# Redoing the set-up of a two-stage transformer kernel: first tokens' norm pinned first, parameters in a later job, rows spread by DMA

## The chip, the cores and the metric

The kernel runs on one core of a Trainium2 chip. The metric is the device time of one execution in microseconds (us). Five engines work side by side: TensorE (PE, matmuls and transposes; PEld is its weight load), VectorE (DVE), ScalarE (ACT), GpSimd (POOL) and SyncE (SP, which here only issues DMAs). ACT and POOL also issue DMAs. An engine runs its own instructions in program order and waits on semaphores for the others.

## The reference, cut to what matters

Two batches of 2048 tokens with 256 features, all float32. The two stages are modulated by a small condition vector `c`:

```python
mod = (_silu(L0_c) @ L0_wmod).reshape(L0_c.shape[0], 6, 1, -1)
sa, ca, ga, sb, cb, gb = (mod[:, 0], mod[:, 1], mod[:, 2], mod[:, 3], mod[:, 4], mod[:, 5])
ga = (2 * (ga >= 0) - 1) * jnp.maximum(jnp.abs(ga), 0.25)
...
h = _layernorm(x, axis=-1) * (1 + ca) + sa
x = x + ga * _L0_attn_ref(h, ...)      # 3 layers: causal linear attention (random features), MLP
h = _layernorm(x, axis=-1) * (1 + cb) + sb
x = x + gb * _L0_ffn_ref(h, ...)       # 2 layers: windowed softmax attention, gated MLP
```

Of the six modulation vectors, only `sa` and `ca` are needed before the first attention layer. `ga` is first needed when a block of tokens leaves the third layer, `sb` and `cb` just after that, and `gb` in the second stage.

## The kernel before, in words

The first stage (from line 207) cuts each batch into blocks of 256 tokens: 8 blocks for each of 2 batches, 16 in all. A block (`favor_block`, line 664) is loaded (`load_x`, line 214, tile `xin`, three buffers), normed (`normed`, line 344: statistics `bs` and `mv` on DVE, a logarithm and an exponential `rs` on ACT, then `dn` on DVE), turned to feature-major (`turned`, line 361: four PE transposes `ntp`, then ACT applies the modulation and writes `h`), and passes three layers (`favor_layer`, line 396). In a layer, PE makes queries and keys `pq` (line 409) and values `pv` (425), the random features `pu` (448), transposes `tk` (484), scores `sc` (495), state updates `su` (515), the denominator `den` (543), the numerator `nd` (554, 567), the output projection `po` (597), and the MLP `pf` and `acc` (619, 630). The residual `hres` of a layer is `dn` times a row plus a row (`scaled`, line 372, on POOL); these rows are parameters that must stand in all 128 partitions, and they are kept in the tile `brow`: 18 rows of 256 numbers. The second stage (from line 692) follows and is not touched.

What sets the order. PE's instructions in the first stage are put in order by hand: `planned` (line 90) runs up to four blocks as generators at once, always takes the one that is due first, and each `yield` states the PE time of the step and the delay until the next may start. `manual_schedule` at line 688 makes PE keep that order. The other engines' orders are made by the framework's scheduler. In the built program PE's order is: 20 transposes for `brow`, the 24 matmuls of the modulation (`pm`, line 295), 16 more transposes for `brow`, the four `ntp` transposes of each of the first four blocks (0,0), (1,0), (0,1) and (1,1) (batch, block), and only then `pq` of the first block. The third and fourth block's `xin` are loaded by the queue of SP, in which all three layers' weights, 3 MB (3072 KB) each, stand ahead of them (line 246). DMAs of SP and ACT use eight completion semaphores in turn, so a DMA is issued only when the one eight before it has landed.

The set-up in the span of line 224 to 338: `wmod` is loaded in two halves (SP and ACT), then `x` of the first two blocks, then weights; POOL's queue loads `bvb` (a bias row that is repeated over the partitions, 384 KB) and eight small pieces of `om_rep`. The modulation needs `sg` (silu of `c`) and all of `wmod`. `spread` (line 271) widens two parameter rows at a time on DVE, transposes the four pieces on PE, and copies them to `brow` on ACT: nine rounds. `omt` (lines 322 to 338) are feature matrices for three layers on DVE.

Of the kernel before, what the change touches and what calls it, by code (L numbers as in the profile page):

```python
# [39 lines left out]
def block_kernel(ctx: ExitStack, tc: tile.TileContext, t: dict, out: bass.AP):  # L40
# [19 lines left out]
    nc.sync.dma_start(cst, t["consts"])  # L60
# [11 lines left out]
    mhalf = const.tile([P, 16], F32, name="mhalf")  # L72
    nc.gpsimd.memset(mhalf, -0.5)
    mod = const.tile([P, 6, KT, B], F32, name="mod")
    omt = const.tile([P, LA, 2, 4, 2, 8], F32, name="omt")
    bvb = const.tile([P, LA, D], F32, name="bvb")
    nc.gpsimd.dma_start(bvb, t["bv"].partition_broadcast(P))
# [129 lines left out]
    with ExitStack() as c1:  # L207
        wp = c1.enter_context(tc.tile_pool(name="wA", bufs=1))
        psum = c1.enter_context(tc.tile_pool(name="psA", bufs=1, space=PSUM))
        brow = wp.tile([P, NROW, D], F32, name="brow")  # L210
        hp = c1.enter_context(tc.tile_pool(name="hA", bufs=3))
        work = c1.enter_context(tc.tile_pool(name="workA", bufs=2))

# [10 lines left out]
        with tc.tile_pool(name="pro", bufs=1) as pro:  # L224
            wmod = pro.tile([P, KT, 6 * D], F32, name="wmod")
            for kt in range(KT):
                (nc.scalar if kt else nc.sync).dma_start(wmod[:, kt, :], t["wmod"][kt * P : (kt + 1) * P, :])
            early = {b: load_x(b, 0) for b in range(B)}
            om_rep = pro.tile([P, LA, 8], F32, name="om_rep")
            for h in range(8):  # L230
                nc.gpsimd.dma_start(om_rep[16 * h : 16 * h + 16], t["omega"].rearrange("l d m -> d l m"))
            W = {}
            for l in range(LA):
                pool = shared if l < 2 else wp
                wa = pool.tile([P, ROOM], F32, tag=f"wa{l}", name=f"wa{l}")
                wb = pool.tile([P, ROOM], F32, tag=f"wb{l}", name=f"wb{l}")
                for room, at, name, kts, width in (
                    (wa, KT * DFF, "Wq", KT, D),
                    (wa, KT * DFF + KT * D, "Wk", KT, D),
                    (wb, NF * D, "Wv", KT, D),  # L240
                    (wb, NF * D + KT * D, "Wo", KT, D),
                    (wa, 0, "W1", KT, DFF),
                    (wb, 0, "W2", NF, D),
                ):
                    w = room[:, at : at + kts * width].rearrange("p (k n) -> p k n", k=kts)
                    (nc.scalar if (name, l) == ("Wq", 0) else nc.sync).dma_start(
                        w, t[name][l].rearrange("(k p) n -> p k n", p=P)
                    )
                    W[name, l] = w

            cv = vec[:, V_C : V_C + KT * B]
            sg = pro.tile([P, KT * B], F32, name="sg")
            nc.scalar.activation(sg, cv, AF.Exp, scale=-1.0)
            nc.vector.tensor_scalar(sg, sg, 1.0, None, ALU.add)
            nc.vector.reciprocal(sg, sg)
            nc.vector.tensor_tensor(sg, sg, cv, ALU.mult)

            cols = pro.tile([P, NROW, KT], F32, name="cols")

            def col(i, *parts):  # L260
                op = parts[2] if len(parts) > 2 else ALU.add
                if len(parts) == 1:
                    nc.vector.tensor_copy(cols[:, i, :], parts[0])
                else:
                    nc.vector.tensor_tensor(cols[:, i, :], parts[0], parts[1], op)

            def va(l, name):
                o = V_A + l * VA_N + VA[name]
                return vec[:, o : o + KT]

            def spread(lo, hi):
                for i in range(lo, hi, 2):
                    wide = pro.tile([P, 2 * KT, P], F32, tag="wide", name="wide", bufs=2)
                    nc.vector.tensor_copy(
                        wide,
                        cols[:, i : i + 2, :].rearrange("p a k -> p (a k)").unsqueeze(2).to_broadcast(
                            [P, 2 * KT, P]
                        ),
                    )
                    tp = mm_tile("rowtp").rearrange("p (a c) -> p a c", c=P)  # L280
                    for k in range(2 * KT):
                        nc.tensor.transpose(tp[:, k, :], wide[:, k, :], ident)
                    nc.scalar.copy(brow[:, i : i + 2, :].rearrange("p a (k c) -> p (a k) c", c=P), tp)

            for l in range(LA):
                col(R_G1 + l, va(l, "g1"))
                col(R_B1 + l, va(l, "b1"), va(l, "bf2"))
            for l in range(LA - 1):
                col(R_G2 + l, va(l, "g2"))
                col(R_B2 + l, va(l, "b2"), va(l + 1, "bo"))  # L290
            spread(0, R_G0)
            pm = mm_tile("pm")
            for m in range(6 * KT):
                for kt in range(KT):
                    nc.tensor.matmul(
                        pm[:, m * B : (m + 1) * B],
                        wmod[:, kt, m * P : (m + 1) * P],
                        sg[:, kt * B : (kt + 1) * B],
                        start=(kt == 0),
                        stop=(kt == KT - 1),  # L300
                    )
            nc.vector.tensor_copy(mod.rearrange("p a k b -> p (a k b)"), pm[:, : 6 * KT * B])
            for i in (1, 4):
                nc.vector.tensor_scalar(mod[:, i], mod[:, i], 1.0, None, ALU.add)
            for i in (2, 5):
                sgn = pro.tile([P, KT, B], F32, name=f"sgn{i}")
                nc.vector.tensor_scalar(sgn, mod[:, i], 0.0, 2.0, ALU.is_ge, ALU.mult)
                nc.vector.tensor_scalar(sgn, sgn, -1.0, None, ALU.add)
                neg = pro.tile([P, KT, B], F32, name=f"neg{i}")
                nc.vector.tensor_scalar(neg, mod[:, i], -1.0, None, ALU.mult)  # L310
                nc.vector.tensor_tensor(neg, neg, mod[:, i], ALU.max)
                nc.vector.tensor_scalar(neg, neg, 0.25, None, ALU.max)
                nc.vector.tensor_tensor(mod[:, i], sgn, neg, ALU.mult)
            for b in range(B):
                col(R_G0 + b, mod[:, 1, :, b])
                col(R_B0 + b, mod[:, 0, :, b], va(0, "bo"))
                col(R_GE + b, va(LA - 1, "g2"), mod[:, 2, :, b], ALU.mult)
                col(R_BE + b, va(LA - 1, "b2"), mod[:, 2, :, b], ALU.mult)
            spread(R_G0, NROW)


            for hf in range(2):
                own, other = slice(64 * hf, 64 * hf + 64), slice(64 - 64 * hf, 128 - 64 * hf)
                for l in range(LA):
                    nc.vector.tensor_tensor(
                        omt[own, l, hf].rearrange("p h s m -> p (h s) m"),
                        om_rep[own, l, :].unsqueeze(1).to_broadcast([64, 8, 8]),
                        hm2[own, 8 * hf : 8 * hf + 8].unsqueeze(2).to_broadcast([64, 8, 8]),
                        ALU.mult,
                    )  # L330
                    nc.vector.tensor_scalar(omt[own, l, hf], omt[own, l, hf], 0.5, None, ALU.mult)
                    nc.vector.tensor_scalar(
                        omt[other, l, hf].rearrange("p h s m -> p (h s m)"),
                        nhalf[other, 64 - 64 * hf : 128 - 64 * hf],
                        0.25,
                        None,
                        ALU.mult,
                    )

        rp = c1.enter_context(tc.tile_pool(name="rA", bufs=2))  # L340
        fp = c1.enter_context(tc.tile_pool(name="featA", bufs=2))
        sp = c1.enter_context(tc.tile_pool(name="smallA", bufs=2))
# [45 lines left out]
        nc.vector.tensor_reduce(par, hmask.rearrange("p (i q) -> p q i", q=2), AX.X, ALU.add)  # L388
# [5 lines left out]
        turn = [0]  # L394

        def favor_layer(b, n, l, h, hres):
# [45 lines left out]
            yield 5.2, 0.6, "attention"  # L442
            feat = []
# [171 lines left out]
            for f in range(NF + 1):  # L615
                if f < NF:
# [9 lines left out]
                    fr[f] = fp.tile([P, TA], F32, tag="fr", name="fr", bufs=3)  # L626
# [37 lines left out]
        def favor_block(b, n):  # L664
            dn = normed(early.pop(b) if n == 0 else load_x(b, n))
            yield 0.0, 4.0
            h = hp.tile([P, KT, TA], F32, tag="h", name="h0")
            turned(dn, h, lambda k: mod[:, 1, k, b : b + 1], lambda k: mod[:, 0, k, b : b + 1])
            hres = scaled(dn, R_G0 + b, R_B0 + b)
# [18 lines left out]
        with tc.manual_schedule(engines={mybir.EngineType.PE}):  # L688
            planned([favor_block(b, n) for n in range(S // TA) for b in range(B)], 4)
# [628 lines left out]
```

## Time and profile before

| | |
|---|---|
| median of 3 runs | 3013.61 us (3012.41 to 3014.05) |
| the profiled execution | 3012.11 us, of which the span from first to last instruction is 3010.3 us |
| PE busy | 2927.8 us (97%) |
| DVE, ACT, POOL busy | 1679.1 us (56%), 1345.9 us (45%), 1065.0 us (35%) |
| mean granted TensorE clock | 0.992 |
| DMA, whole span | 57.10 MB, mean 19 GB/s |
| DMA, 0 to 50 us | 275 GB/s, busy share 0.81 |
| PE busy, 0 to 50 us | 26.29 us |
| PE busy, 50 to 100 us | 47.96 us |

How to read it: "busy" is time in instructions; "idle before" is the gap ahead of an instruction and what ended it. The clock is the share of full speed that the throttle granted to TensorE. In the list of DMAs, "us to landing" is from issue to the moment that the last byte is confirmed. In the chain of waits each row is a start, a length, and an engine with tile and line, or a DMA, that the end of the program hung on.

### The profile page before, as it was taken

The numbers are of one execution on the slowest core, as the hardware profiler recorded it, in microseconds if no ns is written. First come the engines' busy times: TensorE is split into PE (matmuls) and PEld (weight loads), VectorE is DVE, ScalarE is ACT, GpSimd is POOL, SyncE is SP. The second block draws the span as 40 slices with busy tenths as digits, with TensorE's granted clock in tenths as the row PEclk, the third lists the DMA queues.
The fourth block names the chain that finished last, engine by engine and source line by source line (L and its number), as shares of the span: only waits on it lengthen the run. The fifth ranks groups of instructions, "written<-read, shape, count | busy, mean of one in ns | idle before, by whom it ended". The sixth has DMA issues, their size and how long they took to land.

```text
span 3010.3 us, 49194 instructions
## 1 busy us (share of the span) xinstructions
PE 2927.8 (97%) x19356; PEld 2138.0 (71%) x19356; DVE 1679.1 (56%) x4178; ACT 1345.9 (45%) x3269; POOL 1065.0 (35%) x937
## 2 busy tenths in 40 slices
PE   6999999999999999999996999999999999999999
PEld 5788888888888888788883777775444777776444
DVE  5555565555565555655544777774224777774222
ACT  3333343334443343433333667665114667665211
POOL 2222233222332223322224666663002666663000
PEclk9999999999999999999997999999999999999999
DMA  5000010000100001001012000001000000000011
GB/s 183 1 1 1 1 39 19 1 1 1 36 22 1 1 1 36 22 1 43 16 41 76 1 2 1 1 2 57 0 0 10 20 1 2 1 1 8 28 42 35
DMA packets 37288, 57.10 MB, mean 19 GB/s; under 512 B 3693, under 2 KB 28609, under 8 KB 36545
## 3 DMA queue, kind: packets, MB, share of 16 engines
q1 hardware_dynamic: 36176, 52.37, 5.3%
q8 instruction: 153, 2.51, 0.3%
q0 software_dynamic: 464, 0.54, 0.1%
q10 hardware_dynamic: 416, 1.05, 0.1%
q14 instruction: 79, 0.64, 0.1%
HBM read 41.37 MB, written 12.58 MB: 18 GB/s over the span
## 4 chain that ended last, share of the span: by engine, by line
PE 89%; DVE 4%; ACT 3%; POOL 2%; DMA 1%; issue 1%; SPq 1%; ACTq 0%; DVEq 0%; POOLq 0%
PE acc L630 10%; PE pf L619 10%; PE pqkv L785 10%; PE pg L1130 5%; PE acc L1164 5%; PE pq L409 5%; PE pa L1130 4%; PE av L974 4%; PE sim L881 3%; PE ptp L948 3%; PE po L993 3%; PE sc L495 3%; PE nd L567 3%; PE pu L448 3%; PE pv L425 3%; PE po L597 3%
## 5 line engine op out<-in xcount | busy, mean ns | idle before, releaser
L630 PE MATMUL acc<-wb,fr 128*128 128x256 f32 x1536 | 397.3, 381 | 5.5 <-ACT fr L627 5.1
L619 PE MATMUL pf<-h,wa 128*128 128x256 f32 x1536 | 400.2, 384 | 1.1 <-ACT h L370 0.7
L627 ACT ACTIVATE fr<-pf,vec 128x256 f32<-128x256 f32 x384 | 180.5, 471 | 425.6 <-PE pf L619 424.9
L785 PE MATMUL pqkv<-wqkv,s 128*128 128x512 f32 x768 | 357.9, 602 | 8.2 <-issue 8.2
L501 DVE TENSOR_TENSOR att<-sc,cst 128x512 f32<-128x512 f32 x384 | 238.4, 683 | 157.5 <-PE sc L495 157.5
L630 PEld LDWEIGHTS acc<-wb,fr 128*128 128x128 f32 x1536 | 287.8, 190 | 52.1 <-ACT fr L627 8.6
L379 POOL TENSOR_TENSOR res<-dn,brow 128x512 f32<-128x512 f32 x112 | 144.8, 1292 | 485.4 <-DVE dn L356 483.8
L619 PEld LDWEIGHTS pf<-h,wa 128*128 128x128 f32 x1536 | 275.8, 190 | 55.8 <-issue 19.5
L936 POOL TENSOR_TENSOR pm<-pm,sum 128x1024 f32<-128x1024 f32 (+1 forms) x128 | 235.8, 1842 | 178.2 <-DVE sum L931 178.2
L921 ACT ACTIVATE pm<-pm,mx 128x256 f32<-128x256 f32 (+1 forms) x512 | 249.5, 489 | 58.2 <-DVE mx L913 57.0
L785 PEld LDWEIGHTS pqkv<-wqkv,s 128*128 128x128 f32 x768 | 138.0, 193 | 135.8 <-issue 133.9
L1139 DVE SCALAR_TENSOR_TENSOR ge<-pa,vec,ge 128x512 f32<-128x512 f32 x80 | 60.1, 751 | 298.1 <-PE pa L1130 249.7
L827 POOL TENSOR_TENSOR rot<-raw,rsn_wo 128x512 f32<-128x512 f32 x128 | 160.5, 1275 | 185.4 <-ACT raw L808 185.4
L1138 ACT ACTIVATE ge<-pg,vec 128x512 f32<-128x512 f32 x96 | 65.9, 687 | 325.1 <-PE pg L1130 325.1
L421 ACT ACTIVATE xs<-xs 64x512 f32<-64x512 f32 x192 | 120.7, 629 | 152.1 <-DVE xs L420 142.7
L1130 PE MATMUL pg<-s,w 128*128 128x512 f32 (+1 forms) x384 | 182.2, 597 | 0.0
L1164 PE MATMUL acc<-ge,w 128*128 128x512 f32 (+1 forms) x384 | 182.0, 596 | 0.0
L409 PE MATMUL pq<-h,wa 128*128 128x256 f32 x768 | 175.3, 381 | 0.0
L420 DVE TENSOR_TENSOR xs<-pq,vec 64x512 f32<-64x512 f32 x192 | 132.2, 689 | 76.4 <-PE pq L409 72.6
L409 PEld LDWEIGHTS pq<-h,wa 128*128 128x128 f32 x768 | 146.1, 191 | 21.1 <-issue 1.4
L849 POOL TENSOR_TENSOR qk<-qk,rot 128x1024 f32<-128x1024 f32 x64 | 151.5, 2368 | 0.5
L1130 PE MATMUL pa<-s,w 128*128 128x512 f32 x320 | 150.4, 592 | 0.0
(162 smaller groups left out, 5362.6 us busy)
## 6 DMA issues: line engine op xcount, KB each, us to landing
xin<-in_x_dram SPq DMA_DIRECT2D x32, 256.0 KB, 2.8
x<-res SPq DMA_DIRECT2D x16, 256.0 KB, 2.1
h<-hm SPq DMA_DIRECT2D x16, 256.0 KB, 2.4
s<-h SPq DMA_DIRECT2D x16, 256.0 KB, 5.6
xl<-x SPq DMA_DIRECT2D x8, 512.0 KB, 4.4
out_dram<-res SPq DMA_DIRECT2D x8, 512.0 KB, 3.2
w<-in_w_dram SPq DMA_DIRECT2D x6, 640.0 KB, 4.0
wa<-in_W_dram SPq DMA_DIRECT2D x3, 1024.0 KB, 9.7
```

The costliest lines, as they stand in the source:

```text
L409: nc.tensor.matmul(pq[:, g, :], W[wn, l][:, kt, g * P : (g + 1) * P], h[:, kt, :], start=(kt == 0), stop=(kt == KT - 1),)
L501: nc.vector.tensor_tensor(am, scs[i].rearrange("p g q c -> p (g q) c"), caus.unsqueeze(1).to_broadcast([P, 2 * KT, P]), ALU.mult,)
L619: nc.tensor.matmul(pf, W["W1", l][:, kt, f * P : (f + 1) * P], h1[:, kt, :], start=(kt == 0), stop=(kt == KT - 1),)
L627: nc.scalar.activation(fr[f], pf, AF.Relu, bias=v("bf1", f))
L630: nc.tensor.matmul(acc[:, c, :], fr[f - 1][:, c * P : (c + 1) * P], W["W2", l][:, f - 1, :], start=(f == 1 and c == 0), stop=(f == NF), sk ...
L785: nc.tensor.matmul(pq, s[:, kt * TB + c * P : kt * TB + (c + 1) * P], wqkv[:, kt, i * INNER : (i + 1) * INNER], start=(kt == 0), stop=(kt ...
L827: nc.gpsimd.tensor_tensor(rot[:, :, :, lo : lo + 32], got["raw"][:, :, :, hi : hi + 32], rsn[:, ti, :, lo : lo + 32].unsqueeze(2).to_broad ...
L849: nc.gpsimd.tensor_tensor(got["qk"], got["qk"], got["rot"], ALU.add)
L921: nc.scalar.activation(pm[:, hd, :], pm[:, hd, :], AF.Exp, bias=of("mx", hg)[:, hd : hd + 1], accum_out=of("sum", hg)[:, hd : hd + 1],)
L936: nc.gpsimd.tensor_tensor(pm, pm, of("sum", hg).unsqueeze(2).to_broadcast([P, 4, kw]), ALU.mult)
L1130: nc.tensor.matmul(pt[:m, :], w1[:, kt, off : off + m], hb[:, kt * TB : (kt + 1) * TB], start=(kt == 0), stop=(kt == KT - 1),)
L1164: nc.tensor.matmul(acc[m], w2[:w, f, m * P : (m + 1) * P], g[:w, :], start=(f == 0), stop=(f == NFH - 1),)
```

## The change

The set-up is split in three.

First, `first_norm` is a fixed order of PE, DVE and ACT: `sg`, the eight matmuls that make `sa` and `ca` alone, the parameter columns, the norm of block (0,0), its four transposes, its `h`, two transposes for `brow`, `omt` of the first layer. What `planned` orders is held behind the end of that (`issue_after`).

Second, `rest_of_setup` is one more job of `planned`, in second place among the blocks. It holds the other 16 modulation matmuls, in four steps between the blocks' steps, `omt` of the other two layers, the sign and magnitude of `ga` and `gb`, the last four `brow` rows, and the loads of the third layer's weights, which took their place in SP's queue after the second layer's before.

Third, `spread` no longer widens: one transpose turns up to 20 columns into rows, ACT copies them, POOL's DMA stores them to DRAM, and a second DMA of POOL reads them back with each row repeated over the 128 partitions (4 KB and 10 KB per partition at the start, 512 KB and 1280 KB in all; 4 KB, 512 KB, later).

Loads: SP now issues the identity's 64 KB of `consts` alone, then `x` of the first two blocks, then the rest. ACT's queue loads the first third of `wmod` (512 KB), Wq and Wv of the first layer. The other two thirds of `wmod` (1 MB) follow the first layer's W1 on SP. On POOL `om_rep` comes ahead of `bvb`. `wmod` and the staging tile stand in the room that the third layer's weights use later; so these loads wait for the last modulation matmul, and for the store of the last rows. `hres` of a block's first layer is made after `pv` instead of ahead of `pq` when the block is the first of its batch.

In the built program PE's order is now: 8 `pm`, 4 `ntp` of (0,0), 2 transposes for `brow`, `pq` and `pv` of (0,0), then 8 `ntp` of (1,0) and (0,1), `pu` of (0,0), 4 `pm`, `tk`, `sc`, `su`, 8 `pm`, `sc`, `den`, 4 `pm`, `nd`, and so on. The `ntp` of (1,1) stand beside those of the first block's MLP input, and one transpose for `brow` follows the second block's `pu`. Behind that, PE's order is the same as before, instruction by instruction. On SP, `xin` of block (0,1) follows the second layer's weights.

```diff
-            for kt in range(KT):
-                (nc.scalar if kt else nc.sync).dma_start(wmod[:, kt, :], t["wmod"][kt * P : (kt + 1) * P, :])
-            early = {b: load_x(b, 0) for b in range(B)}
...
+        nc.scalar.dma_start(wmod[:, :, : 2 * D], wmod_in[:, :, : 2 * D])
+        early = {b: load_x(b, 0) for b in range(B)}
+        nc.sync.dma_start(cst[:, P:], t["consts"][:, P:])
...
+        load_weights(0, "Wq", "Wk", "Wv", "Wo")
+        load_weights(0, "W1")
+        nc.sync.dma_start(wmod[:, :, 2 * D :], wmod_in[:, :, 2 * D :])
+        load_weights(0, "W2")
+        load_weights(1, "Wq", "Wk", "Wv", "Wo", "W1", "W2")
...
+        def spread(lo, hi):
+            n = (hi - lo) * KT
+            tp = mm_tile("rowtp")[:n, :P]
+            nc.tensor.transpose(tp, cols[:, lo:hi, :].rearrange("p a k -> p (a k)"), ident)
+            turned_ = turned_cols.pop()[:n]
+            nc.scalar.copy(turned_, tp)
+            nc.gpsimd.dma_start(rows_out[lo * KT : hi * KT], turned_)
+            nc.gpsimd.dma_start(
+                brow[:, lo:hi, :].rearrange("p a d -> p (a d)"),
+                rows_out[lo * KT : hi * KT].rearrange("a c -> (a c)").partition_broadcast(P),
+            )
...
+        def first_norm(normed, turned):
...
+                pm = mm_tile("pm")
+                condition(0, 2, pm)
...
+                dn = normed(early.pop(0))
+                conditioned(0, 2, pm)
+                h = hp.tile([P, KT, TA], F32, tag="h", name="h0")
+                turned(dn, h, lambda k: mod[:, 1, k, 0:1], lambda k: mod[:, 0, k, 0:1])
...
+                spread(R_G0, R_GE)
+                spread(0, R_G0)
+                omega_rows(0)
...
+        def rest_of_setup():
+            yield 0.0, 8.0, "mlp"
+            pm = psum.tile([P, NCA * D], F32, tag="acc", name="pm2", bufs=1)
+            for i in range(2, 6):
+                condition(i, i + 1, pm)
+                yield 1.7, 0.0, "mlp"
+            conditioned(2, 6, pm)
...
+            yield 0.0, 2.5
+            spread(R_GE, NROW)
+            load_weights(2, "Wq", "Wk", "Wv", "Wo", "W1", "W2")
+            yield 0.2, 0.0
...
+            with tc.issue_after(last_first):
+                planned(blocks[:1] + [rest_of_setup()] + blocks[1:], 4)
```

## The prediction, made before the run

> **What bounds the kernel now.** I read the page first: PE is busy for 97% of the span, and of its 40 slices of 75 us only the first and one at the stage change are poor. The change touches the start alone, and behind it PE's order is the same, so what counts is how soon PE gets going for good. The table of busy times by stretch shows where the start is lost (columns: stretch, length, busy us and instructions of PE, PEld, DVE, ACT, POOL, then clock, DMA share, GB/s):
>
> ```profile
> 20.00:25.00 5.00, 4.52 (x22) 4.43 (x21) 0.41 (x3) 0.00 (x0) 0.00 (x0) 1.00 1.07 376
> 25.00:30.00 5.00, 2.79 (x13) 2.62 (x14) 4.27 (x33) 1.57 (x4) 0.00 (x0) 1.00 1.09 352
> 30.00:35.00 5.00, 2.49 (x13) 1.71 (x11) 3.26 (x6) 2.48 (x6) 3.75 (x5) 0.96 1.06 381
> 35.00:40.00 5.00, 0.07 (x1) 0.00 (x0) 0.55 (x2) 1.02 (x2) 3.09 (x3) 0.50 0.87 278
> 40.00:45.00 5.00, 1.70 (x5) 0.87 (x5) 4.34 (x11) 2.02 (x6) 3.48 (x3) 0.50 0.19 54
> ```
>
> The DMA engines are full until 38 us (one-microsecond stretches show it), while no engine is. PE idles from 35 to 42 us. The chain of waits says for what:
>
> ```profile
> 26.29 0.71 SPq L246
> 27.04 12.39 DMA xin<-in_x_dram
> 39.45 0.75 DVE bs L349 x2
> ...
> 45.52 0.90 PE ntp L366 x3
> 46.42 4.42 PE pq L409 x16
> 50.84 1.79 PE pv L425 x8
> 52.63 2.04 PE pu L448 x16
> 54.69 0.61 ACT ft L458
> 55.34 0.66 PE tk L484 x4
> 55.99 1.07 PE sc L495 x16
> 57.07 1.09 PE su L515 x8
> 58.16 2.60 PE sc L495 x16
> ```
>
> The chain does not run through the modulation or `brow`. It runs through the load of `x` of the third block, (0,1), issued at 27.04 behind 9 MB of weights and landed at 39.45. Blocks (0,0) and (1,0) had been transposed by 35 us, but PE's order has all four blocks' `ntp` ahead of the first `pq`. From 46.42 on PE hardly stops: 47.96 of the 50 us from 50 to 100.
>
> **The change, part by part.** First what vanishes from PE's start: 36 transposes become 3 and the first norm needs 8 of the 24 `pm` matmuls. In the timeline the first 20 transposes end at 14.5, the `pm` take 10.24 us to 24.5 and the last 16 transposes 3.65 us from 27.21. All of that lies beside the loads, so shortening it gains nothing by itself. DVE's widening and ACT's nine copies likewise. In the new order, `h` of (0,0) should stand at about 10 to 12 us: `vec` landed at 4.55 before, 256 KB of `x` come early in the queue, and norm, 8 `pm` (3.4 us) and transposes (0.9 us) follow. Then `pq` and `pv` run by about 18 us instead of 46 to 52.6.
>
> Then PE stops. Next in its order are `ntp` of (1,0), which is ready, and of (0,1), whose `x` still stands behind two layers' weights on SP. So the same load is late next; call its landing T. I compare the moment when `pu` of (0,0) starts: 52.63 before.
>
> T: the third layer's 3072 KB (3.146 MB) no longer stand ahead of it. At the rate of 20 to 35 us (376, 352, 381: mean 370 GB/s) that is 8.5 us. Added are POOL's two repeated rows, 1792 KB (1.835 MB) of DMA. Their issue: `brow` columns are copied by about 11 us, POOL is through its 8 `om_rep` issues (0.59 us each), `bvb` and two 1.84 us memsets by then; the store lands some 5 to 7 us later (`om_rep` took 5.5 to 7.8), and the reading back runs from about 20 to 30 us, inside the wait for T. Here a rule speaks against the change. In the stretches when `bvb`, the like transfer, moved beside SP's and ACT's, the rates were 401, 230 and 283 GB/s (5 to 8 us; mean 305). The Trainium skill, "DMA: Bandwidth & Descriptors", section "Issuing engines are not separate DMA queues", says that DMAs issued on POOL end up on the same 16 DMA engines and interleave with the others. The row agrees: the third queue raised no total. By the rule the repeat is paid by T; were POOL's queue apart, it would cost nothing. Its price: by the mean of the nearest stretch 1.835/0.305 = 6.0 us; at best 5.0 (370 GB/s); at worst 8.0 (230). I take 6.0. Moving `wmod`, Wq, Wv, `consts` and `om_rep` changes no bytes ahead of T. T = 39.45 - 8.5 + 6.0 = 36.95, say 36.9.
>
> From T to `pu`: statistics, logarithm, exponential and first half of `dn` took 2.0 us before (39.45 to 41.42), then four transposes at half clock 1.2 us: 3.3 with a semaphore. `pu` starts at T + 3.3.
>
> What PE does behind it, beyond before: 16 `pm` matmuls, two passes each, at 10.24/48 = 0.213 us: 6.8 us. Four stand between `pu` and `tk`, where PE waited 0.69 us for `ft` (timeline), eight between `su` and the second `sc`, which took 2.60 instead of 1.07 since DVE had to free its PSUM. So 0.7 + 1.5 is cover and 4.6 us is paid; without the cover it would be 6.8. The transpose for `brow` hides in the same wait of the second block, the `ntp` of (1,1) in the 0.66 us wait for `h` at 78.07. But DVE norms (1,1) just ahead of that: two statistics (0.74) before the first block's `dn`, whose transposes PE waits for; cover 0.5: 0.2 us paid, at most 0.8.
>
> Clock: PE idles from about 18 us to T + 2, so its clock falls, as it did at 34.8 before. Before, dense work started at 45.5 and the clock was back at 48.2; that fell on `pq` (4.42 instead of 3.65 us). Now it falls on `ntp`, `pu` and `pm`. The Trainium skill, "TensorE: Matmul & The Clock Gate", Part 1, has the clock restored after a busy window of about 3.4 us that runs free. By the row 2.7 us at half clock cost 1.35; by the rule, as an estimate, the restart can miss a window and wait up to two, 6.8 us, which costs 3.4. I take 4.1 us at half clock, 2.05 us, of which 0.45 is in the transposes already: 1.6.
>
> Other steps at nothing: 18 small DVE instructions of the later job (0.07 us apart, 1.3 us) stand ahead of `aT`, while PE has the second block's `pq` and `pv` (5.4 us). POOL's store of the last rows waits for ACT's copy; behind it stand `res` and the second block's `z`, wanted by `den` at 82.03: z ended at 77.25, `res` takes 2 times 1.27, issue 0.5, so 1.5 us remain. The reading back waits on POOL for the store (5 us); behind it are `res` and state updates, wanted much later. The third layer's loads now wait on SP for the last `pm` and that store, about 75 us; behind them is one `x` of a later block end, and a POOL addition waits for that to about 80, before POOL's next `z`, wanted at about 101. The weights themselves are first used at 263.9.
>
> Sum: gain = 52.63 - (36.9 + 3.3) - 4.6 - 0.2 - 1.6 = 6.0, i.e. 43.0 - T with rounding. The profiled execution, 3012.1 (span 3010.3), would fall to 3006.1; the median of the runs, 3013.6, stands 1.5 above it, so I forecast 3007.6. The sum rounds at the border of what the measurement can tell, 0.2% or 6 us.
>
> **The rivals.** *POOL's repeat costs T nothing*, because its bytes fill gaps or end outside the wait. For: two queues together reached 413 GB/s at 3 to 4 us, more than SP's alone. Against: the DMA share lies at 1.0 to 1.1 from 8 to 38 us, so there are no gaps. T = 30.9, gain 12.1: 3001.5. Chance 0.18.
>
> *The room is taken up again*: `x` of (0,1) still lands at 39 to 42, by small rows of `wmod` and slower interleaving. For: the fall to 230 GB/s beside POOL. Gain 1 to 4: 3011. Chance 0.11.
>
> *It is not what PE waits for*: if PE needed only the first block, it would go on from 18 us. Gain 52.6 - 18 - 4.6 = 30: 2984. The order with `ntp` of (0,1) ahead of `pu` speaks against it. Chance 0.02.
>
> *Slower*: POOL's large pieces (8 or 16 rows' worth against SP's 1 KB) take two thirds of the engines' time, and repeating one DRAM row is slow: `bvb` needed 7.5 us to landing for 384 KB, which makes 35 us of 1792 KB. SP's last 4 MB at 20 us would then run at a third of 370 GB/s: 33 us, T = 53, 10 us slower: 3024. It decides from T = 43 on (no gain), and is over 0.2% slower from T = 49. Against it: while `bvb` moved, the total was never below 230 GB/s. Chance 0.04.
>
> The likeliest, T between 35.5 and 39.4, has 0.65: 3006.1 to 3010.
>
> **How the numbers follow.** Within the likeliest case the price of the repeat (5 to 8), the clock (0.9 to 2.9) and DVE's 0.8 put the gain at 3.5 to 7.5, half of it on each side of 6. Faster: 0.35 + 0.18 + 0.02 = 0.55. Same: 0.30 + 0.11 = 0.41. Slower: 0.04. The range takes in the first rival and the slow end: 3001.5 to 3010.5; outside remain the small mishaps, 30 us of gain and the slow case.
>
> **What would show it.** Right: `pq` of (0,0) before 20 us, then PE idle to T + 2 with `xin` on the chain; T near 37; the clock at half from the low 20s to about 42; `pu` near 40; second `sc` without its wait; the same gaps from 100 us on; the third layer's loads near 55 and 75 us with nobody waiting. Wrong: T at 31 or over 40; a wait of PE for `brow` or `res` at `po`; a gap at `den` by a late `z`; or PE stopped before `pq` by Wk or `om_rep`.

## The result, and the profile after

The changed kernel takes 3008.73 us (median of 22 runs, 3005.76 to 3013.69), the kernel before 3013.80 in the same comparison (22 runs, 3009.94 to 3015.80): a ratio of 0.9984, 95% interval 0.9977 to 0.9990, or 5.1 us. The profiled execution took 3008.91 us (span 3007.1, mean granted clock 0.989), 3.2 us less than the profiled one of before. The runs of the changed kernel are spread by 8 us, and the spread goes with the mean granted clock: 0.990 in the three at 3006, 0.986 in the one at 3013.7.

The same five stretches as before, from the changed kernel's table of busy times by stretch, in the same columns:

```profile
20.00:25.00 5.00, 0.10 (x1) 0.00 (x0) 0.60 (x2) 1.06 (x3) 0.00 (x0) 0.90 1.06 393
25.00:30.00 5.00, 0.00 (x0) 0.00 (x0) 0.00 (x0) 0.00 (x0) 0.00 (x0) 0.50 1.02 396
30.00:35.00 5.00, 0.00 (x0) 0.00 (x0) 0.55 (x2) 0.00 (x0) 0.00 (x0) 0.50 0.94 297
35.00:40.00 5.00, 3.42 (x16) 2.10 (x18) 1.15 (x5) 1.86 (x5) 3.16 (x3) 0.50 0.21 53
40.00:45.00 5.00, 5.00 (x47) 3.58 (x44) 4.71 (x4) 1.44 (x3) 4.91 (x4) 0.89 0.01 3
```

The modulation, the first norm, and `pq` and `pv` of block (0,0) are done by 19.7 us. Then every engine stands still for about 15 us while the DMA engines stay full. The chain of waits says for what, and what it costs to start again:

```profile
17.91 16.51 DMA xin<-in_x_dram
34.45 0.75 DVE bs L408 x2
...
36.58 1.13 PE ntp L425 x4
37.71 3.56 PE pu L510 x16
41.27 0.98 PE pm L310 x8
...
44.91 1.68 PE pm L310 x16
46.59 3.44 PE sc L557 x15
50.03 2.00 PE den L605 x4
52.04 1.50 PE pm L310 x8
53.54 1.86 PE nd L629 x32
55.40 1.15 PE nd L616 x4
56.55 1.80 PE nd L629 x32
58.35 3.65 PE pq L469 x16
...
74.03 1.96 PE pf L681 x8
...
83.38 3.65 PE pq L469 x16
```

The same part of the chain before the change, from `den` of (0,0) on:

```profile
60.75 1.06 PE den L543 x4
61.81 1.01 PE nd L567 x32
62.83 0.64 PE nd L554 x4
63.47 1.01 PE nd L567 x32
64.48 3.65 PE pq L409 x16
...
78.07 2.02 PE pf L619 x8
...
87.48 3.65 PE pq L409 x16
```

It is still the load of `x` of block (0,1), now landed at 34.45 instead of 39.45, and `pu` of (0,0) starts at 37.71 instead of 52.63. But of this lead of 14.9 us only 6.1 are left at the next block's `pq` (58.35; 64.48 before), and 4.0 at the first block's `pf` (74.03; 78.07). At `pq` of (0,1) the lead is 4.1 (83.38; 87.48). So 10.9 us are given back within 40 us, and the experiments have two questions: what set T, and where the 10.9 went. Compare lengths in the two chains: `pu` takes 3.56 instead of 2.04, the second `sc` 3.44 instead of 2.60, and `nd` 4.81 (three rows) where before had 2.66 (1.01, 0.64, 1.01). The clock fell a second time, from 47.9 to 58.2, in the midst of what is recorded as busy work.

One line of the chain explains itself only in the timeline of DVE and POOL. First the changed kernel, from the start of POOL's residuals (start, length of the group, count, idle before):

```profile
36.84 2.49 POOL L438 TENSOR_TENSOR res<-dn,brow 128x512 f32<-128x512 f32 x2 [18.87 <-DVE dn L415]
40.29 1.95 DVE L526 TENSOR_SCALAR qe<-ft,par 128x512 f32<-128x512 f32 x2 [3.54 <-ACT ft L520]
42.16 3.37 DVE L532 TENSOR_TENSOR_SCAN z<-ft,zero 128x256 f32<-128x256 f32 x2
```

Then the same two steps of DVE in the kernel before, where POOL was idle beside them:

```profile
54.52 0.88 DVE L464 TENSOR_SCALAR qe<-ft,par 128x512 f32<-128x512 f32 x2 [1.10 <-ACT ft L458]
55.32 1.27 DVE L470 TENSOR_TENSOR_SCAN z<-ft,zero 128x256 f32<-128x256 f32 x2
```

POOL's order has the residual of block (0,1) first, which needs that block's norm. So all residuals run behind T, from 36.84 to 45, and beside them DVE needs 5.3 us instead of 2.1 for the two steps that PE's scores wait for.

### The profile page after: what moved, and what is told of

The parts are those of the page before. It is cut to its first block, busy times and chain, and to the rows that moved or that the text cites. A ratio compares the mean times of both kernels' runs of the same rounds, so it can differ in the third digit from the quotient of the medians.

```text
span 3007.1 us, 49118 instructions
## 1 busy us (share of the span) xinstructions
PE 2926.8 (97%) x19323; PEld 2135.3 (71%) x19323; DVE 1677.9 (56%) x4170; ACT 1341.0 (45%) x3263; POOL 1068.9 (36%) x942
## 4 chain that ended last, share of the span: by engine, by line
PE 89%; DVE 4%; ACT 3%; POOL 2%; issue 1%; DMA 1%; SPq 0%; ACTq 0%; POOLq 0%; DVEq 0%
PE acc L692 11%; PE pf L681 10%; PE pqkv L854 10%; PE pg L1199 5%; PE acc L1233 5%; PE pq L469 5%; PE pa L1199 4%; PE av L1043 4%; PE sim L950 3%; PE ptp L1017 3%; PE po L1062 3%; PE sc L557 3%; PE nd L629 3%; PE pu L510 3%; PE po L659 3%; PE pv L485 3%
## 5 line engine op out<-in xcount | busy, mean ns | idle before, releaser
L692 PEld LDWEIGHTS acc<-wb,fr 128*128 128x128 f32 x1536 | 288.4, 190 | 52.6 <-ACT fr L689 8.6
```

Of the source, the lines that this page charges most:

```text
L692: nc.tensor.matmul(acc[:, c, :], fr[f - 1][:, c * P : (c + 1) * P], W["W2", l][:, f - 1, :], start=(f == 1 and c == 0), stop=(f == NF), sk ...
```

## The experiments

My theory ("waits"): T is set by SP's queue and by POOL's repeat; what is lost behind `pu` is PE waiting for DVE, which POOL slows. The rival ("thin"): the 16 small `pm` matmuls in the stream are what costs, by their own time and since they keep TensorE too little occupied, so that the clock falls again. Each experiment edits the changed kernel, and each comparison has its own runs of the kernel before (medians 3014.1 to 3014.4 us; 3013.8 for the changed kernel). Where a run is called faster than the changed kernel, the two medians are subtracted, so half a microsecond of it can be the comparison.

**Is the gate T, and nothing else?** `x` of (0,1) is issued right behind the first two.

```diff
-        early = {b: load_x(b, 0) for b in range(B)}
+        early = {(b, 0): load_x(b, 0) for b in range(B)}
+        early[0, 1] = load_x(0, 1)
...
-                dn = normed(early.pop(b) if n == 0 else load_x(b, n))
+                dn = normed(early.pop((b, n)) if (b, n) in early else load_x(b, n))
```

> The changed kernel, with the load of x of block (0,1) issued on SP directly behind the x of the first two blocks, ahead of all weights; PE's order stays. If that load is what PE waits for (gate), its statistics start at 9 to 12 us instead of 34.45, pu of (0,0) at 20 to 22 instead of 37.7, and everything behind it 14 to 17 us earlier; the time falls from 3008.7 to 2993 to 2997. If weights or the rows in brow are what PE needs next anyway, PE stops again at pu, po or pf until 30 to 35 us and the gain is 5 us or less.

Measured: 2990.81 us, ratio 0.9922 (0.9909 to 0.9934): 17.9 us faster than the changed kernel, somewhat more than I expected. Its chain of waits has no `xin` any more:

```profile
16.89 7.61 DMA brow<-rows_out
24.64 2.50 POOL res L439 x2
...
30.40 1.23 POOL z L543
31.67 2.07 PE den L606 x4
```

`pu` starts at 19.6, and what is late next is the repeat: the residuals wait for `brow` until 24.64, POOL's `z` stands behind them, and PE's `den` waits for it. The gate is shown.

**What does the repeat cost T?** The reading back is replaced by a constant, so the parameter rows are left out.

```diff
-            nc.gpsimd.dma_start(
-                brow[:, lo:hi, :].rearrange("p a d -> p (a d)"),
-                rows_out[lo * KT : hi * KT].rearrange("a c -> (a c)").partition_broadcast(P),
-            )
+            nc.gpsimd.memset(brow[:, lo:hi, :], 1.0)
```

> The changed kernel without POOL's repeating read into brow: a memset of 1.0 on POOL stands in its place, so the rows of parameters are left out. If the 1792 KB are paid by the wait for the third x, its landing falls from 34.45 by 5 us (4 to 6) to about 29.5, and the time by as much. If POOL's bytes fill gaps, the landing stays within 1 us of 34.45.

Measured: 3004.60 us (3001.15 to 3006.58), ratio 0.9966 (0.9953 to 0.9978). In its chain of waits, the third `x` landed at 29.62 instead of 34.45:

```profile
29.62 0.75 DVE bs L405 x2
```

So 1.835 MB cost T 4.8 us, 382 GB/s, and not nothing; in the time 4.1 us.

**Are the small matmuls the loss?** The 16 `pm` stand behind `pv`, where PE is idle.

```diff
-            yield 0.0, 8.0, "mlp"
+            yield 0.0, 3.0, "mlp"
...
                 condition(i, i + 1, pm)
+            yield 0.1, 1.3, "mlp"
+            for _ in range(4):
                 yield 1.7, 0.0, "mlp"
```

> The changed kernel, with all 16 later modulation matmuls together behind pv of (0,0), where PE waits for the third x anyway; PE's order is else the same. pu of (0,0) should stay at 37.7. Theory thin (matmuls of two columns count as little activity, and that is why the clock falls again at 48 us): no second fall, pq of (1,0) at about 51 instead of 58.4, 7 us faster. Rival waits (the second fall comes from PE's waits for DVE's att): the clock falls again, pq of (1,0) at 54 to 55, about 4 us faster. If the matmuls were covered, nothing changes.

Measured: 3007.99 us (14 runs, 3004.23 to 3010.03), ratio 0.9979 (0.9971 to 0.9987): 0.7 us under the changed kernel, which is not clear of the spread. In the median both expectations missed. The profiled execution, 3004.52, is one of the three fastest, and it looks otherwise. Its chain of waits, then its stretch from 50 to 55 us and that of the changed kernel (the clock is the third number from the end):

```profile
37.50 3.64 PE pu L512 x16
...
52.60 3.65 PE pq L471 x16
```

```profile
50.00:55.00 5.00, 5.00 (x79) 4.21 (x76) 2.11 (x4) 1.32 (x2) 0.00 (x0) 1.00 0.01 3
50.00:55.00 5.00, 5.00 (x45) 4.45 (x44) 3.11 (x20) 1.32 (x2) 0.00 (x0) 0.50 0.05 11
```

The clock came back later than in the changed kernel (45.9 instead of 41.1) and then did not fall again, as "thin" had it, though DVE's two steps took 1.96 and 3.36 us beside POOL. `pq` of (1,0) starts at 52.60, between the two expectations. Whether the clock fell in the executions near the median is not known, since none of them was traced.

**Is it POOL beside DVE?** The residual of (0,1), too, is made after `pv`, so that the other blocks' residuals on POOL no longer wait for T.

```diff
-            if n > 0:
+            if n > 1:
                 hres = hres()
```

> The changed kernel, with the first residual of block (0,1) too made only when that block reaches it, so POOL's first res no longer waits for dn of (0,1); those of (0,0) and (1,0) can run while PE waits for x. Theory waits: qe and z on DVE no longer run beside POOL (1.95 and 3.37 us become about 0.9 and 1.3), att starts 2.5 to 3 us earlier, the second fall of the clock at 48 us does not come, 4 to 5 us faster. Theory thin: att comes earlier, but the clock still falls near 48 us, gain at most 1.5 us.

Measured: 3005.49 us (10 runs, of which nine at 3005.05 to 3007.11), ratio 0.9975 (0.9965 to 0.9984): 3.2 us faster than the changed kernel, somewhat under what "waits" gave. The profiled execution was the tenth, 3013.98: its clock stayed at half from 21.7 to 62.6, so its trace doesn't stand for the median.

**Does a warm clock help?** Two tries with matmuls that nobody reads. Fourteen of 512 columns behind `pv`:

> The changed kernel with 14 matmuls of 512 columns, whose result nobody reads, behind pv of (0,0): about 12 us of PE's 16 us wait for the third x at full clock, so no work is added to the path. Theory clock (the start that the change gains is partly lost because PE comes back at half clock and stays there, for the lone first block gives it too little to do): pu takes 2.0 instead of 3.6 us, most of the half-clock time between 37 and 58 us goes, pq of (1,0) starts 3 to 6 us earlier than 58.4 and the time falls by 3 to 6 us. Rival (the half clock costs little, the rest is waits and the 16 small matmuls): at most 1.5 us.

Measured: 3009.46 us (21 runs), ratio 0.9985 (0.9978 to 0.9991). This tells nothing: the matmuls ran from 19.60 to 31.78, PE came back at 36.9, and the clock had fallen again at 34.4 (`pu` 3.43 us). Then the same fourteen together with the 16 `pm` behind `pv`:

> The 16 later modulation matmuls moved into PE's wait for the third x, as in the run that moved them alone (which gained 0.7 us in the median), and the 14 unread matmuls behind them. Theory clock: moving them gained so little because PE then stayed at half clock longer; with the clock kept up pq of (1,0) starts at 49 to 51 instead of 58.4, 7 to 9 us faster than the changed kernel. Rival: no more than the moved matmuls alone, 1 to 2 us.

Measured: 3008.26 us (16 runs), ratio 0.9977 (0.9969 to 0.9984), 0.5 us under the changed kernel. They ran until 37.04 and made `pu` 1.8 us late, but it ran at full clock (1.95 us). Yet with a warm clock and no small matmul in the stream PE waited for `ft` (0.70), `qe` (0.50) and `att` (1.63), since DVE's two steps again took 1.98 and 3.28 us beside POOL. The second `sc` took 3.86, and the clock fell at 48.2, as in the changed kernel:

```profile
47.14 3.86 PE L565 MATMUL sc<-qe,ft 32*128 32x256 f32 x16 [1.63 <-DVE att L571]
```

So the second fall does not need the small matmuls, against "thin". Nor are DVE's slow steps enough for it: in the profiled execution with `pm` behind `pv` alone they were as slow.

**Is it the norm of (1,1) between `pu` and `pf`?** Its start is put off.

```diff
-            yield 0.2, 0.0
+            yield 0.2, 6.0
```

> The changed kernel with the start of block (1,1) put off by 6 us of planned time, so that DVE norms it after the first block's MLP input. If DVE's norm of (1,1) is what keeps PE at 65 to 74 us, pf of the first block follows pu of the second by 6.5 us as before the change, not by 8.6, and the time falls by about 2 us. If PE only finds another wait, nothing changes within 1 us.

Measured: 3008.73 us (21 runs), ratio 0.9984 (0.9978 to 0.9991), the changed kernel's own. The profiled execution took 3013.07, with the clock at half from 21.5 to 62.5, ahead of the part that matters here. From `pu` of (1,0) to `pf` it is still 8.1 us (6.5 before, 8.6 in the changed kernel). The edit moved the transposes of (1,1) behind `pf` in PE's order, but not the norm of (1,1) in DVE's order, where half of it still stands ahead of `att`:

```profile
75.17 1.37 DVE L415 TENSOR_SCALAR dn<-xin,mv,rs 128x256 f32<-128x256 f32 x1 [0.60 <-ACT rs L412]
76.46 2.47 DVE L563 TENSOR_TENSOR att<-sc,cst 128x512 f32<-128x512 f32 x4
77.24 1.97 PE L681 MATMUL pf<-h,wa 128*128 128x256 f32 x8 [2.29 <-issue]
```

The profile names no releaser for `pf`, but the kernel's text does: `pf` and the scores `sc` take turns in the same four buffers of PSUM, the memory that PE writes to (lines 553 and 679 of the changed kernel), and a buffer comes free when an `att` has read its scores. In the changed kernel and in all twelve variants of it, `pf` starts 0.77 to 0.78 us after DVE starts `att`, whose first instruction takes 0.69. Before the change `att` started 2.05 us ahead of `pf` (76.02), which waited for ACT's `h`. And from `pu` to ACT's `h` the changed kernel takes 5.94 us, the same as before, so all of the 2.1 us lie behind `h`. The expectation fell because the edit didn't put off what it was meant to put off; the wait is for DVE, which comes late to `att`.

**Both cures of the loss together.** `pm` behind `pv`, and the late residual of (0,1).

> On the changed kernel, both cures together: the 16 matmuls of the modulation stand in PE's long wait behind pv, and the residual of block (0,1) is made later, so that POOL works less beside DVE. If what is lost behind pu is PE's wait for DVE beside POOL plus the small matmuls, the two gains add: the clock does not fall a second time, pq of (1,0) starts near 51 instead of 58.4, and the time is 3000 to 3003. If the clock falls again by the luck of its windows whatever is waited for, or PE waits for the next engine instead, it is about 3005, as with the late residual alone.

Measured: 3002.96 us (3002.03 to 3003.90), ratio 0.9965 (0.9952 to 0.9977): 5.8 us faster than the changed kernel, where the two alone gave 0.7 and 3.2. DVE's steps in the timeline, with POOL idle beside them:

```profile
40.03 0.88 DVE L528 TENSOR_SCALAR qe<-ft,par 128x512 f32<-128x512 f32 x2 [3.54 <-ACT ft L522]
41.74 1.27 DVE L534 TENSOR_TENSOR_SCAN z<-ft,zero 128x256 f32<-128x256 f32 x2 [0.82 <-ACT ft L522]
```

and its chain of waits:

```profile
37.45 3.64 PE pu L512 x16
...
44.58 2.59 PE sc L559 x16
47.17 1.06 PE den L607 x4
48.23 1.01 PE nd L631 x32
...
50.90 3.65 PE pq L471 x16
...
64.27 2.71 DVE dn L417 x2
67.67 1.97 PE pf L683 x8
```

The lengths are those of before (`sc` 2.6, `den` 1.06, `nd` 1.01) except `pu`, which runs at half clock. From `pu` to the next `pq` it takes 13.45 us: before 11.85, in the changed kernel 20.64; the 1.6 that remain are `pu`'s. The expectation is borne out, to the place (51 expected, 50.90) and the time, and the two cures give more together than the 3.9 us of their sum. Since both causes are out, this run does not tell them apart. Behind it 3.2 us are still lost to `pf`: there DVE's two `dn` of (1,1) take 2.71 us, beside two products on POOL that take 3.32.

**The cold restart by itself.** The late residual, `pm` where they were, and 18 unread matmuls, which last until PE goes on.

> On the changed kernel with the late residual (3005.5): 18 matmuls of 512 columns whose result nobody reads are put into PE's wait behind pv, 0.87 us each at half clock, from 19.6 to about 35, so that the clock has been restored when PE goes on. If the cold restart costs what the chain shows (pu 3.6 instead of 2.0, transposes 1.1 instead of 0.5, the rest behind waits), 2 to 3 us are gained: 3002.5 to 3004. If the work behind pu is bound by DVE and ACT anyway, nothing is gained: 3005 to 3006.

Measured: 3002.76 us (3001.05 to 3003.30), ratio 0.9962 (0.9950 to 0.9975): 2.7 us faster than the late residual alone. In its chain of waits:

```profile
37.22 1.88 PE pu L517 x16
...
50.01 3.65 PE pq L476 x16
```

The clock stays up from 15.8 to 67.0 in its trace; the unread matmuls took 0.87 us each at full clock, not at half as I had written. So the cold restart costs 2.7 us. And the 16 `pm` are in the stream here, 3.45 us of them; from `pu` to `pq` it takes 12.8 us against 11.85 before, so with DVE free of POOL they cost 0.9.

This kernel and the one with fourteen unread matmuls and `pm` behind `pv` set the two theories against each other with the clock up when `pu` starts. With DVE beside POOL and no small matmuls in the stream, `pu` to `pq` takes 17.1 us, the second fall of the clock included, and the time is 3008.26 (lowest 3003.66); with the small matmuls and DVE free, 12.8 us and 3002.76 (highest 3003.30). Of the 5.5 us between the times, 2.3 are the later start of `pu` there. "Waits" names the larger part of the loss.

**A better kernel?** On top of the early `x`, three tries to get POOL's `z` from behind the residuals: the late residual of (0,1); the residual of (0,0) made only just ahead of `po`; both.

> Third x ahead of the weights and the first residual of (0,1) made late, together. With the third x early, the chain runs over POOL: z of (0,0) waits in POOL's queue behind residuals that wait for brow (24.6 us). With fewer residuals ahead of z, den of (0,0) starts 2 to 3 us earlier than 31.7, so 2988 to 2990 against 2990.8. If POOL's first residual waits for brow all the same, no change within 1 us.

> The early third x (2990.8), and the first block's residual made only just ahead of po. In the kernel with the early x, POOL's z of (0,0) started at 30.36 behind four residual steps that waited for the repeated rows until 24.64, and PE waited 3.69 us for it at den. One residual's steps of 2 times 1.26 us are still ahead of z in POOL's order, and a state that waits for DVE's sum at 27.2: den starts about 1 us earlier (30.5), the time is about 2989.7. If PE waits for something else instead, 2990.8.

> As the one before, and the residual of block (0,1) is late too: only one step of 1.26 us and the state stand ahead of z on POOL. By POOL's order den starts at 29.2 instead of 31.67, 2.5 us earlier: 2988.3. If the residuals that are now later slow DVE's norm, as they did with the late residual on the early x (2992.6), the gain is lost again behind den: 2990 to 2992.

Measured: 2992.57, 2991.12 and 2993.49 us; ratios 0.9928 (0.9915 to 0.9942), 0.9925 (0.9911 to 0.9938) and 0.9933 (0.9921 to 0.9946). None beats the early `x` alone. `den` did come earlier: 30.88, 31.50 and 29.25 instead of 31.67. The last kernel's chain of waits shows how that is lost:

```profile
29.25 2.08 PE den L604 x4
...
49.48 3.31 POOL res L439 x2
52.82 2.75 DVE dn L416 x2
```

The residuals that were put off now run beside DVE's norms, and `pf` starts at 56.3 against 55.3.

Where the kernels stood, by the start of PE's groups in their traces:

| | `pu` (0,0) | `pq` (1,0) | `pf` | `pq` (0,1) | this execution | median |
|---|---|---|---|---|---|---|
| before | 52.6 | 64.4 | 78.1 | 87.4 | 3012.1 | 3013.8 |
| changed | 37.6 | 58.3 | 74.0 | 83.3 | 3008.9 | 3008.7 |
| `pm` in the gap | 37.4 | 52.5 | 68.3 | 77.6 | 3004.5 | 3008.0 |
| no repeat | 33.8 | 54.3 | 70.0 | 79.3 | 3001.2 | 3004.6 |
| late residual, warm | 37.2 | 49.9 | 66.8 | 77.8 | 3001.1 | 3002.8 |
| `pm` in the gap, late residual | 37.4 | 50.8 | 67.7 | 77.0 | 3003.9 | 3003.0 |
| early `x` | 19.6 | 39.5 | 55.3 | 66.3 | 2991.1 | 2990.8 |

The lead over before at `pq` of (0,1) is 4.1, 9.8, 8.1, 9.6, 10.4 and 21.1 us; the same executions are 3.2, 7.6, 11.0, 11.1, 8.2 and 21.1 us shorter than the profiled one of before. The start carries the result, to within 3 us.

## Why the prediction was right, and where its steps were not

**The number** (3007.6 for 3008.73) came out, and in part by luck. The time lies in the range of the case that I called likeliest (3006.1 to 3010), but T, 34.45, lies ahead of the 35.5 to 39.4 that define this case: PE got going sooner than predicted and then lost more. The terms were off, some beyond the bounds that I gave them, in opposite directions:

| step | predicted | measured |
|---|---|---|
| lead at `pu` of (0,0) | 12.4 | 14.9 |
| lost from there to `pq` of (1,0) | 4.6 + 1.6 | 8.8 |
| lost from there to `pf` | 0.2 | 2.1 |
| lead at `pf` | 6.0 | 4.0 |

Between the two profiled executions the gain was 3.2 us, not 6.0; that the medians differ by 5.1 is what brings the number so near.

**What bounds the kernel: right.** T was the gate, before and after, and the early `x` shows it. I took the load's place in the queue as given and weighed only what stood ahead of it; the trace before already said that moving the load itself is worth more than all else in the change.

**T: mechanism right, size off by 2.5 us.** The repeat was priced at 6.0 and cost 4.8; it ran at 382 GB/s where I took 305 from the stretches with `bvb`. My better bound, 370, was the nearer. The rest, 1.3 us, lies in the other term: without the repeat `x` landed 9.8 us earlier than before the change, where I had 8.5 for the third layer's weights. No run takes these weights out alone. (One misreading made no difference: the two memsets on POOL take 1.84 us together, not each.) The rule that POOL's DMAs share the engines with the others holds here: they were full throughout, and T moved by the bytes. From T to `pu` it took 3.26 us (3.3 predicted).

**`pm`: the term was mis-sized, and the cover was not what I took it for.** I priced a pass at 0.213 us from the trace before. At 14 to 24 us there, PE ran at half clock, which the clock column doesn't show: it reads 1.00 ahead of the first stretch of clock that the trace holds. In the late residual's trace, where the column reads 0.50, 16 such passes took 3.41 us, again 0.213 each; in the changed kernel, at 1.00, they took 1.85 us (at 44.74). The 16 matmuls took 0.98 + 1.68 + 1.50 = 4.16 us, not 6.8. Taking them out gained 0.7 us in the median and 0.9 us is their cost where DVE is free; the rest was hidden behind PE's waits for DVE.

**The clock: the first restart as thought, the second fall not foreseen.** PE came back at 36.58 and the clock at 41.1; I had taken 4.1 us at half clock. It cost `pu` 1.5 us, and 2.7 us in all by the warm run. What I had no term for is POOL's residuals beside DVE, PE's waits from that, and a clock that falls again: `sc`, `den` and `nd` take 0.84 + 0.94 + 2.15 = 3.9 us more. I had named POOL's residuals only as something that stands ahead of `z`. The page "SBUF — State Buffer" of the Trainium skill, section "SBUF: two separate sides", says that certain DVE instructions and GpSimd's exclude each other from a shared pair of ports, for whole instructions. The rows agree in kind: one `qe` took 0.98 us instead of 0.44, one scan 1.69 instead of 0.64, beside additions and products on POOL of 1.25 us, which became 1.45 to 1.54 themselves. By the rule, each of the four could wait for one such instruction, up to 5 us as an estimate; it was 3.2. That it is a lock and not a sharing is not shown.

**DVE's norm of (1,1): wrong in size.** I had 0.2, at most 0.8. It was 2.1. I had only the transposes that wait for DVE; `pf` waits as well for a buffer that DVE's `att` sets free, and `att` comes behind the norm. In the changed kernel POOL's next residual runs beside DVE there: `z` takes 2.27 us instead of 1.27, and the two `dn` of (1,1) 1.61 instead of 0.72. No experiment takes that residual away from there, so POOL's part in the 2.1 is argued.

**What was to be seen.** `pq` before 20 us, `xin` on the chain, `pu` two or three us sooner than said, half clock from 24.0: so it was. The third layer's loads were issued at 53.57 and 70.49, and nobody waited for them; `brow` and the late `z` held up nobody. The second `sc` did not lose its wait, which was the sign that I had asked for and should have given a price. What sets off the second fall within stretches that are recorded as busy stays open. It came with the small matmuls in the stream and without them, in the changed kernel, the one without the repeat and both tries with fourteen unread matmuls, while PE waited for DVE; it did not come by 60 us in the profiled executions of the two kernels at 3003, where DVE was free, nor in that of `pm` behind `pv` alone, where DVE was slow. And in the profiled execution of the late residual DVE was free (0.89 and 1.27 us), and the clock stayed at half through 26 us of work without a gap. Nor is it settled why the lead of 4.1 us at `pq` of (0,1) is 3.2 in the two profiled executions and 5.1 in the medians; the spread of the clock is large enough for both.

**The rivals.** That the repeat costs T nothing is refuted by 4.8 us; that the room is taken up again, by T; that POOL's large pieces starve SP's, by T and by 352 to 461 GB/s while they ran. That PE needs only the first block was wrong for this order of PE; with the third `x` early it comes close (2990.8 against my 2984), and `brow` is then what is late.

## What to carry to other kernels

When a start hangs on one load, first count the bytes ahead of that load in its queue: 256 KB moved to the front gave 18 us here, over three times the whole rearrangement. When a gate opens earlier, list everything that was waiting for the same gate on *other* engines, for it will now run beside the work that you freed; here residuals on POOL, the first of them needed 20 us later, slowed DVE by 3 us ahead of the scores, and putting them off with the small matmuls out of the way gave 5.8. An edit to PE's order leaves the other engines' orders as they are, so look in the trace at whether the step really moved there. And take a duration from a row only after looking at whether its passes ran at the clock that you mean.

## What the runs showed that I had not expected

- Plain additions and products on POOL slow DVE's steps by 2.2 (`qe`) and 2.7 times (`z`). Put off, they do the same to the next steps: two `dn` took 2.71 to 2.75 us instead of 0.72.
- The clock can stay at half for 41 us (21.7 to 62.6) in an execution whose other runs took 7 to 9 us less; the runs of one kernel are spread by 8 to 10 us (three of the kernels here), more than the change is worth.
- The stretches of clock in the traces are multiples of 3.41 us: in the changed kernel 17.1 at half, 6.8 at full, 10.2 at half; 41.0 at half in the late residual.
- The clock column reads 1.00 ahead of the first recorded stretch (17.2 us in the changed kernel) although PE is at half: `pq` of 16 passes took 6.59 us at 11.35, and 3.65 later.
- Unread matmuls keep the clock up only if they last until PE is needed: ending 5 us early brought nothing, ending 2 us early 2.7 us.
